# Earlier due times for the two variance transposes of an attention, and closer chunks in one normalisation

## The chip, the cores and the metric

The kernel runs on one core of a Trainium2 chip. The metric is the device time of one execution in microseconds (us). Before the change the median of three runs is 2762.81 us, and the runs lie between 2762.28 and 2766.79. All data is fp32.

## The reference

Eight images of 768 channels and 32x32 = 1024 tokens go through two residual layers. The core of it, shortened:

```python
def _L0_conv_ref(x, W_qkv, W_proj, b_proj):          # layer 0
    q, k, v = (qkv[0], qkv[1], qkv[2])               # 12 heads of 64
    var_v = jnp.var(v, axis=-1, ddof=1, keepdims=True)
    var_k = jnp.var(k, axis=-1, ddof=1, keepdims=True)
    scores = var_v @ jnp.swapaxes(var_k, -2, -1) * scale
    attn = jax.nn.softmax(scores, axis=-1)
    out = attn @ v
    out = out @ W_proj.T + b_proj
...
def _L1_conv_ref(feature, conv_w, conv_b):           # layer 1
    # 28 shifted products of the normalised features, summed over channels
    corr = jnp.stack([jnp.sum(feat_pad[:, :, r:h + r, cc:w + cc] * feat_n, axis=1) for r, cc in _offsets()], axis=1)
    x = jnp.concatenate([feature, corr], axis=1)
    out = jnp.einsum('bchw,oc->bohw', x, conv_w) + conv_b[None, :, None, None]
...
x = x + _L0_conv_ref(_gn(x), ...)                    # _gn: group norm, 32 groups
x = x + _L1_conv_ref(_gn(x), ...)
```

The queries are not used. A score is a product of one number for each query token (the head variance of v) and one for each key token (the head variance of k), so the attention needs no matmul for its scores: a row of value variances, spread over 128 partitions, goes through an exponential whose scale for each partition is a key variance.

## The kernel before

**The stages of an image.** The images are called 0 to 7. For each image the kernel runs: group norm; the projections to K and V, in two halves of six heads (`KeysValues`); the variances of each half (`spread`); the attention, in six pairs of heads, three to a half (`Pair`, `Attention`); the output projection with the residual and its statistics (`project`), which gives f; group norm of f; and layer 1 on f: the Gram products of the correlation (`Corr`, L1006) and the 1x1 convolution with its residual (`Conv`). Layer 1 of image b − 1 runs mixed with the attention of image b. The projections and the convolution are cut into units by a Strassen scheme, six matmuls each: 1.94 us for a unit of K and V, 2.57 us for one with a weight tile (wt) by TensorE's own records. In the profile the unit matmuls all stand at L342, since one helper issues them.

**The hand-over from projection to attention.** After the last unit of a half, `spread` works out, on VectorE (all of its instructions are recorded at L146), the scaled variance of k (km), its largest value (top, and most on GpSimd, L616) and that of v (vm), each 128 tokens by 48 (six heads by eight token tiles). Then two jobs follow.
- `values` calls `to_rows` on vm: TensorE transposes it (ptv, L501), VectorE copies it out (rsv), and the SyncE queue stores it to DRAM (vdr<-rsv, L504). From there `Pair.rows` loads one row for each head, spread over 128 partitions: bc<-vdr, 512 KB each, L665.
- `keys` computes nk, the key scale (six VectorE instructions). For the first half a job `rows` follows, 0.5 us after VectorE is free by the planner's count, which does the same for nk: ptk, rsk, kdr<-rsk, and bk<-kdr at L665.

**The attention of a pair.** For each of eight key tiles t and both heads, ScalarE computes ex = exp(bc · nk) (L674, 128x1024), and TensorE adds four products with v into av (L699), in blocks of four steps (32 records). The denominators come in one of two ways. For pairs 0, 1 and 2 ScalarE also computes exp(bk · vm) with a sum over its row (junk, L684); the sums are inverted (inv), transposed (it, L808), copied (ir), stored (di<-ir, L812) and loaded spread over partitions (rd<-di, L771). For pairs 3, 4 and 5 VectorE adds up the ex tiles (acc). From the second image on these three are the summed ones; in the first image pair 0 is one of them too. At last VectorE multiplies the finished pair by rd (v<-v,rd). There is one rd buffer, so the load for a pair waits until the pair before it is multiplied.

**What sets the order.** The program is written in one pass by a planner, `Clock`. `later.after(us, job)` puts a job at the planner's time plus us; `later.after_dve(us, job)` counts from the time at which the planner expects VectorE to be free. When the time comes, the job's instructions are appended to the engines' programs. These times are the planner's own and never wait on the chip: they only decide in which order each engine, and the SyncE queue with all of the large DMAs, runs its instructions. On the chip each engine runs its own list in that order, and between engines there are semaphores. The DMAs of the SyncE queue use eight completion semaphores in turn, so an issue also waits for the landing of the DMA eight issues before it.

**What stands around the hand-over of the second half.** Conv.start (L1103) loads the residual of layer 1 from DRAM in six row groups (x<-x1d), which are the accumulators of the convolution; VectorE's x<-x,bconv_sb,x and x<-y,bconv_sb,x add a unit's result and the bias to one. `thirds` and `fourth` of the convolution are the sums t2f, f<-f and t4f on VectorE. wt are the streamed weight tiles (L306, 196 KB), kv the ones of the projections (L279, 576 KB).

**What stands around it in the first half.** Gram products with their copies (win<-gr) and stores (windowed<-win, L1016) lie between the units of the second half. win copies, ptv, ptk and the inverse's transposes share the two PSUM buffers of the pool `smp`.

**The residual's normalisation.** `project` collects the group norm statistics of f. `apply` (inside it) calls `Norm.apply` (L457), which normalises the image in six chunks of 128x1024 (f<-f), each due `apart` us after the one before. Except for the last image f is overwritten in place, after a copy of each row group has been stored for layer 1's residual (x1d<-f).

Of the kernel before, what the change touches and what calls it, by code (L numbers as in the profile page):

```python
# [14 lines left out]
NB, C, H, W = 8, 768, 32, 32  # L15
# [136 lines left out]
def two_layers(ctx, tc, x, wkv, wproj, bproj, wconv, wcorr, bconv, out):  # L152
# [30 lines left out]
    later = clock  # L183
# [16 lines left out]
    def image_tile(pl, tag, name):  # L200
        return pl.tile([P, J, N], F32, tag=tag, name=name)
# [218 lines left out]
    def gn_tile(name):  # L420
        return st.tile([P, 2 * J, 6], F32, tag="bn", bufs=2, name=name)

    def gn_stats(bn, t, j, hf):
        vector.bn_stats(out=bn[:, 2 * j + hf, :], in_=t[:, j, hf * HF : (hf + 1) * HF])
# [61 lines left out]
    def head_m2(bn, m2, name):  # L486

        d = st.tile([P, MT * HH], F32, tag="hd", name=f"hd{name}")
        s = st.tile([P, MT * HH], F32, tag="hs", name=f"hs{name}")
        by_tile = [a.rearrange("p (t h) -> p t h", h=HH) for a in (d, s)]  # L490
        vector.tensor_tensor(d, bn[:, :, 1], bn[:, :, 4], ALU.subtract)
        vector.tensor_tensor(s, bn[:, :, 2], bn[:, :, 5], ALU.add)
        vector.tensor_tensor(d, d, d, ALU.mult)
        vector.scalar_tensor_tensor(
            m2.rearrange("p h t -> p t h"), by_tile[0], float(HD // 4), by_tile[1], ALU.mult, ALU.add
        )

    def to_rows(cols, dr, name):

        pt = small(f"pt{name}")  # L500
        nc.tensor.transpose(pt[0 : MT * HH, 0:P], cols.rearrange("p h t -> p (h t)"), ident)  # L501
        rs = work([MT * HH, P], f"rs{name}")
        vector.tensor_copy(rs, pt[0 : MT * HH, 0:P])
        nc.sync.dma_start(out=dr.rearrange("h (t p) -> (h t) p", p=P), in_=rs)  # L504

    class KeysValues:
# [47 lines left out]
        def unit(self, half, d, n, g, p):  # L554
            b = self.b
            if n == 0:
                self.make_sums(half, (2 * d, 2 * d + 1))
            s = self.sums[g]
            a = {1: self.block(g, 0, 0), 2: self.block(g, 0, 1), 4: self.block(g, 1, 1)}
            a.update({5: s[:, 0], 6: s[:, 1], 7: s[:, 2], 3: s[:, 3]})  # L560
            w = kv_stream.tiles[b, half, d, p]
            pairs = [(a[p][:, k, :], w[:, k, :]) for k in range(JH)]
            banks.product(g, p, KV_US, KW, pairs, lambda ps: self.take(half, g, p, ps))
            if p not in [q for _, q in PAIR[n + 1 :]]:
                kv_stream.done((b, half, d, p))
            if d == 1 and n == len(PAIR) - 1:
                self.over = half == 1
                later.after(KV_US + 0.5, lambda: later.after_dve(0.0, lambda: self.spread(half)))
# [39 lines left out]
        def spread(self, half):  # L608
            b = self.b
            name = f"{b}_{half}"  # L610
            km2 = st.tile([P, HH, MT], F32, tag="km2", bufs=2, name=f"km2{name}")
            head_m2(self.bn["k", half], km2, f"k{name}")
            top = st.tile([P, HH], F32, tag="top", name=f"top{name}")
            vector.tensor_reduce(top, km2, AX.X, ALU.max)
            most = st.tile([P, HH], F32, tag="most", name=f"most{name}")
            nc.gpsimd.partition_all_reduce(most, top, P, bass_isa.ReduceOp.max)  # L616
            m2 = st.tile([P, HH, MT], F32, tag="vm2", bufs=4, name=f"vm2{name}")
            head_m2(self.bn["v", half], m2, f"v{name}")
            nk = st.tile([P, HH, MT], F32, tag="nk", bufs=4, name=f"nk{name}")
            kdr, vdr = [dpool.tile([HH, N], F32, tag=f"{kind}dr", name=f"{kind}dr{name}") for kind in "kv"]  # L620
            for of, new in ((self.m2, m2), (self.nk, nk), (self.kdr, kdr), (self.vdr, vdr)):
                of.append(new)

            def values():
                to_rows(m2, vdr, f"v{name}")
                ready.add(("v", b, half))

            def keys():
                for h in range(HH):
                    vector.tensor_scalar(  # L630
                        nk[:, h, :], km2[:, h, :], most[:, h : h + 1], HD ** -0.5 / (HD - 1) ** 2,
                        ALU.subtract, ALU.mult,
                    )
                ready.add(("nk", b, half))
                if not set(SUMMED[b > 0]).issuperset(range(3 * half, 3 * half + 3)):
                    later.after_dve(0.5, rows)

            def rows():
                to_rows(nk, kdr, f"k{name}")
                ready.add(("k", b, half))  # L640

            later.after_dve(2.5, values)
            later.after_dve(3.5, keys)


    class Pair:
# [78 lines left out]
        def sum_up(self):  # L725
# [14 lines left out]
            def out():  # L740
                ds = denpool.tile([P, HF], F32, tag="den", name=f"ds{b}_{hp}")
                act_copy(0.55, ds, den)
                for at in range(4):
                    nc.sync.dma_start(
                        out=dr[0][at // 2 : at // 2 + 1, at % 2 * HF : (at % 2 + 1) * HF], in_=ds[32 * at : 32 * at + 1, :]
                    )
                later.after(6.0, spread)
# [437 lines left out]
    def project(b, ots):  # L1185
        f = first_f[0] if b == 0 else image_tile(fpool, "f", f"f{b}")
        for n, us in ((0, 0.0), (1, 0.5), (3, 1.5), (4, 3.0), (2, 12.0), (5, 14.0)) if b else ():
            later.after(us, lambda n=n: nc.sync.dma_start(out=f[:, n, :], in_=xv[b, :, n, :]))
        bn = gn_tile(f"bn2_{b}")
        if b + 1 < NB:  # L1190
            x1_dram[b] = dpool.tile([P, J, N], F32, tag="x1", name=f"x1d{b}")
        left = {(i, hf) for i in range(J) for hf in range(2)}

        def finished(i, hf):
            gn_stats(bn, f, i, hf)
            left.remove((i, hf))
            if b + 1 < NB and (i, 1 - hf) not in left:
                nc.sync.dma_start(out=x1_dram[b][:, i, :], in_=f[:, i, :])
            if not left:
                later.after(0.1, normalise)  # L1200

        def normalise():
            norm = Norm(bn, f"b{b}")
            later.after_dve(0.3, norm.means)
            later.after_dve(3.0, norm.spreads)

            def apply():
                to = f if b + 1 < NB else image_tile(xnpool, "xn", "f_last")
                layer1.append((to, f))
                norm.apply(to, f, ("f", b), 2.0 if b + 1 < NB else 0.0)  # L1210

            later.after_dve(5.0, apply)

        sums = TokenSums(f"o{b}", ots[:JH], ots[JH:])
        clock.wait(("ot", b, JH - 1), ready=ready)
        sums.first()
        wide = Wide("p", f"p{b}", f, bproj_sb, sums.operand, finished)
        late = True
        for n, (us, _, unit) in enumerate(wide.units()):
            if n == 4:  # L1220
                clock.wait(("ot", b, HP - 1), ready=ready)
            if late and n > 1 and ("ot", b, HP - 1) in ready:
                late = False
                sums.second()
                later.after(3.0, sums.thirds)
                later.after(8.0, sums.fourth)
            unit()
            clock.pass_time(us)
# [55 lines left out]
    for b in range(NB + 1):  # L1284
# [6 lines left out]
        if b:  # L1291
# [3 lines left out]
            f, acc = layer1[b - 1] if b > 1 else first_f * 2  # L1295
# [66 lines left out]
```

## Time and profile before

| what | value |
|---|---|
| median of the runs | 2762.81 us (2762.28 to 2766.79) |
| the profiled execution | 2773.49 us, of which its span is 2771.8 us |
| granted TensorE clock, mean | 0.993 |
| TensorE busy | 2712.3 us, 98% of the span |
| VectorE busy | 1664.1 us, 60% |
| ScalarE busy | 1362.3 us, 49% |
| GpSimd busy | 307.0 us, 11% |
| DMA moved | 451.85 MB, mean 163 GB/s |
| TensorE waiting for ex (av<-ex,v) | 12.3 us in 15 waits, the longest 5.0 us |

The span goes from the first to the last instruction of the profiled execution. Busy time counts the records of an engine; loading weights overlaps with matmuls and is counted apart. A line of a timeline gives start and duration in us from the span's start, engine, source line, operation, the tiles as out<-in, sizes, the number of records joined to it, and in brackets the idle time just before it and what ended that. A line of the SyncE queue (SPq) is a DMA's issue and not its landing. A line of the waits gives the engine, what it was about to run, what it waited for, and then the total, the number of waits and the longest.

### The profile page before, as it was taken

How to read it: one execution, taken by the hardware profiler on the slowest of the kernel's cores; microseconds unless marked ns; L12 is line 12 of the kernel's file. 1: busy time of each engine (PE TensorE's matmuls, PEld its weight loads, DVE VectorE, ACT ScalarE, POOL GpSimd, SP SyncE). 2: the span in 40 equal slices, each digit the busy share in tenths (PEclk: the TensorE clock that was granted, in tenths of full speed). 3: DMA queues.
4: the chain of work that ended last, by engine and by line, in shares of the span. 5: the costliest groups of instructions: out<-in, count | busy, mean ns of one | idle time of the engine just before them, and what ended most of it. 6: DMA issues, size and time to landing. Idle time of an engine off the chain costs nothing.

```text
span 2771.8 us, 28821 instructions
## 1 busy us (share of the span) xinstructions
PE 2712.3 (98%) x9063; PEld 1277.7 (46%) x9063; DVE 1664.1 (60%) x4163; ACT 1362.3 (49%) x1814; POOL 307.0 (11%) x350
## 2 busy tenths in 40 slices
PE   6999999999999999999999999999999999999999
PEld 3543454335643455434554346533465334653353
DVE  4858734685447854478534884358743587446853
ACT  1398078520596106970079701886019850298400
POOL 3420101002200031000310012100121001110000
PEclk9999999999999999999999999999999999999999
DMA  8764454545554545536456365563654536535323
GB/s 302 280 227 150 142 189 122 163 165 160 175 150 143 187 154 157 165 128 204 150 158 189 97 203 168 149 181 91 228 175 130 182 97 222 171 113 170 117 73 95
DMA packets 324579, 451.85 MB, mean 163 GB/s; under 512 B 59794, under 2 KB 245890, under 8 KB 324426
## 3 DMA queue, kind: packets, MB, share of 16 engines
q1 hardware_dynamic: 322618, 444.88, 50.8%
q10 hardware_dynamic: 1808, 5.11, 0.5%
q8 instruction: 73, 1.20, 0.2%
q14 instruction: 80, 0.66, 0.1%
HBM read 380.44 MB, written 67.38 MB: 162 GB/s over the span
## 4 chain that ended last, share of the span: by engine, by line
PE 74%; issue 10%; DMA 5%; ACT 5%; DVE 4%; SPq 1%; POOL 1%; DVEq 0%; POOLq 0%; ACTq 0%
PE x L342 29%; PE av L699 17%; PE y L342 14%; PE z L342 8%; ACT ex L674 3%; PE gr L1006 2%; DMA rd<-di 2%; ACT junk L684 2%; DMA bc<-vdr 1%; DVE dn L146 1%; PE den L732 1%; PE z L936 1%; PE x L936 1%; PE den L782 1%; DVE cs L146 0%
## 5 line engine op out<-in xcount | busy, mean ns | idle before, releaser
L674 ACT ACTIVATE ex<-bc,nk 128x1024 f32<-128x1024 f32 x768 | 834.5, 1138 | 493.6 <-DMA bc<-vdr 271.3
L699 PE MATMUL av<-ex,v 128*64 128x512 f32 x3072 | 709.1, 601 | 12.3 <-ACT ex L674 12.3
L684 ACT ACTIVATE junk<-bk,vm 128x1024 bf16<-128x1024 f32 x368 | 420.5, 1143 | 41.9 <-DMA bk<-kdr 35.6
L699 PEld LDWEIGHTS av<-ex,v 128*64 128x64 f32 x3072 | 218.7, 138 | 473.9 <-issue 394.4
L146 DVE TENSOR_TENSOR acc<-acc,ex 128x1024 f32<-128x1024 f32 x350 | 401.6, 1212 | 0.0
L209 ACT COPY kp<-x 128x384 f32<-128x384 f32 x28 | 13.3, 479 | 558.1 <-PE x L342 558.1
L342 PE MATMUL y<-kv,s 128*128 128x384 f32 x768 | 267.8, 489 | 2.6 <-DMA kv<-kvs 2.6
L342 PE MATMUL x<-kv,xn 128*128 128x384 f32 x768 | 263.9, 490 | 4.4 <-DVE xn L146 3.3
L342 PE MATMUL x<-kv,s 128*128 128x384 f32 x768 | 262.2, 489 | 3.3 <-POOL s L546 3.3
L342 PEld LDWEIGHTS x<-kv,xn 128*128 128x128 f32 x768 | 145.1, 191 | 108.6 <-issue 14.3
L342 PEld LDWEIGHTS x<-kv,s 128*128 128x128 f32 x768 | 145.4, 191 | 104.1 <-issue 6.8
L342 PEld LDWEIGHTS y<-kv,s 128*128 128x128 f32 x768 | 142.4, 190 | 102.1 <-issue 8.7
L1006 PE MATMUL gr<-f 128*128 128x227 f32 (+1 forms) x672 | 131.8, 346 | 0.0
L342 PE MATMUL z<-kv,xn 128*128 128x384 f32 x384 | 130.1, 488 | 0.0
L342 PE MATMUL x<-v,wt 128*128 128x512 f32 x288 | 130.0, 596 | 0.0
L1006 PEld LDWEIGHTS gr<-f 128*128 128x128 f32 x672 | 121.2, 190 | 18.7 <-issue 6.2
L146 DVE TENSOR_TENSOR v<-y,v 128x128 f32<-128x128 f32 x180 | 40.9, 282 | 136.5 <-PE y L342 136.5
L342 PE MATMUL x<-f,wt 128*128 128x512 f32 x252 | 115.4, 598 | 0.1
L452 POOL TENSOR_TENSOR rstda<-vea,neghalf 128x1 f32<-128x1 f32 x8 | 4.8, 597 | 930.2 <-DVE vea L146 930.2
L546 POOL TENSOR_TENSOR s<-xn 128x384 f32<-128x384 f32 x64 | 68.5, 1080 | 309.6 <-PE x L342 219.4
L146 DVE BATCH_NORM_STATS2 vbn<-v 128x6 f32<-128x64 f32 x720 | 101.7, 210 | 0.0
L146 DVE COPY acc<-ex 128x1024 f32<-128x1024 f32 x50 | 33.7, 703 | 107.6 <-ACT junk L684 36.8
(170 smaller groups left out, 2925.0 us busy)
## 6 DMA issues: line engine op xcount, KB each, us to landing
kv<-kvs SPq DMA_DIRECT2D x128, 576.0 KB
kv<-in_wkv_dram SPq DMA_DIRECT2D x96, 576.0 KB
bc<-vdr SPq DMA_DIRECT2D x96, 512.0 KB
f<-in_x_dram SPq DMA_DIRECT2D x48, 512.0 KB
bk<-kdr SPq DMA_DIRECT2D x46, 512.0 KB
x1d<-f SPq DMA_DIRECT2D x42, 512.0 KB
x<-x1d SPq DMA_DIRECT2D x42, 512.0 KB
out_dram<-x SPq DMA_DIRECT2D x84, 256.0 KB
```

Of the source, the lines that this page charges most:

```text
L146: return getattr(self.engine, name)(*args, **kw)
L209: nc.scalar.copy(to, at)
L342: nc.tensor.matmul(t, lhsT=lhsT, rhs=rhs, start=p in FIRST and k == 0, stop=stop and k == len(pairs) - 1, skip_group_check=True,)
L452: nc.gpsimd.tensor_tensor(self.rstd, ve, neghalf[:, 0:1], ALU.pow)
L546: nc.gpsimd.tensor_tensor(self.sums[g][:, 0], a[g][2], a[g][3], ALU.add)
L674: nc.scalar.activation(ex, self.bc[e], AF.Exp, scale=self.kv.nk[self.half][:, h, t : t + 1])
L684: nc.scalar.activation(junk, self.bk[e], AF.Exp, scale=self.kv.m2[self.half][:, h, t : t + 1], accum_out=self.sums[:, e, t : t + 1],)
L699: nc.tensor.matmul(self.av[e * HD : (e + 1) * HD, hf, :], lhsT=self.vt[:, t, e, :], rhs=exs[e][:, hf * HF : (hf + 1) * HF], start=t == 0, ...
L732: nc.tensor.matmul(den[at * 32 : (at + 1) * 32, :], lhsT=ones[:, 0:32], rhs=self.acc[e][:, hf * HF : (hf + 1) * HF], start=True, stop=True,)
L782: nc.tensor.matmul(den[e * HD : (e + 1) * HD, :], lhsT=ones, rhs=self.acc[e][:, at], start=True, stop=True)
L936: nc.tensor.matmul(t, lhsT=wcorr_sb[at, i, :], rhs=cs[at, tokens, :], start=False, stop=True, skip_group_check=True)
L1006: nc.tensor.matmul(ps[:, :n], lhsT=f[:, j, t * P : (t + 1) * P], rhs=f[:, j, t * P : t * P + n], start=j == 0, stop=j == J - 1,)
```

## The change

Three numbers change. `values` is due 1.0 us instead of 2.5 us after VectorE's expected end, and `keys` 2.2 us instead of 3.5 us, in all images but the first. And the six chunks of the residual's normalisation in `project` are due 1.0 us apart instead of 2.0 us where b is 0; b counts from 0, so this is the first image's residual. It is described in words as the second image's, whose layers run while that residual is used. The other images keep 2.0 us, and the last one 0.

```diff
@@ -639,8 +639,8 @@
                 to_rows(nk, kdr, f"k{name}")
                 ready.add(("k", b, half))
 
-            later.after_dve(2.5, values)
-            later.after_dve(3.5, keys)
+            later.after_dve(1.0 if b else 2.5, values)
+            later.after_dve(2.2 if b else 3.5, keys)
 
 
     class Pair:
@@ -1207,7 +1207,7 @@
             def apply():
                 to = f if b + 1 < NB else image_tile(xnpool, "xn", "f_last")
                 layer1.append((to, f))
-                norm.apply(to, f, ("f", b), 2.0 if b + 1 < NB else 0.0)
+                norm.apply(to, f, ("f", b), (2.0 if b else 1.0) if b + 1 < NB else 0.0)
 
             later.after_dve(5.0, apply)
```

No instruction is added or removed: every engine has the same number of instructions before and after, in another order.

## The prediction

> **What bounds the kernel now.** I read the busy times first: TensorE is busy 98% of the span.
>
> ```profile
> PE 2712.3 (98%) x9063; PEld 1277.7 (46%) x9063; DVE 1664.1 (60%) x4163; ACT 1362.3 (49%) x1814; POOL 307.0 (11%) x350
> ```
>
> The change adds and removes no instruction, so it can only move TensorE's idle and slow stretches. The view of what TensorE waited for shows how much there is:
>
> ```profile
> PE av L699 <- ACT ex L674: 12.3, 15, 5.0
> ...
> PE ct L1052 <- DVE dn L146: 5.2, 7, 3.1
> ...
> PE ptv L501 <- DVE vm L146: 1.8, 5, 0.5
> ```
>
> Only the first row belongs to the softmax hand-over, 12.3 us. It is too small, because a block that waits between its own records stretches them. A block of four steps (32 records, av) takes 7.02 us where nothing waits (image 4, 1440.80 to 1447.82). By TensorE's timeline the first block of pair 3 takes, start to next start, 15.06 (image 1), 10.51, 10.50, 10.63, 10.48, 8.81 and 8.27 us (images 2 to 7). Over 7.02 that is 8.04, 3.49, 3.48, 3.61, 3.46, 1.79 and 1.25, together 25.1 us; images 2, 3, 4 and 5 also start it 0.86, 1.6, 0.14 and 0.35 us late. This is the loss that the change can reach. TensorE, then VectorE, the DMA issues and ScalarE of image 4 show what makes it:
>
> ```profile
> 1501.07 0.29 PE L501 MATMUL ptv<-ident,vm 128*48 128x128 f32 x1 [0.41 <-DVE vm L146]
> ...
> 1520.56 6.08 PE L699 MATMUL av<-ex,v 128*64 128x512 f32 x22 [0.33 <-ACT ex L674]
> 1526.88 2.97 PE L699 MATMUL av<-ex,v 128*64 128x512 f32 x8 [0.24 <-ACT ex L674]
> ```
> ```profile
> 1503.00 0.75 DVE L146 SCALAR_TENSOR_TENSOR x<-x,bconv_sb,x 128x512 f32<-128x512 f32 x1 [1.99 <-DMA x<-x1d]
> 1503.67 1.88 DVE L146 TENSOR_TENSOR f<-f 128x512 f32<-128x512 f32 x3
> 1505.47 0.74 DVE L146 SCALAR_TENSOR_TENSOR x<-y,bconv_sb,x 128x512 f32<-128x512 f32 x1
> 1508.78 1.23 DVE L146 TENSOR_TENSOR v<-v,rd 128x1024 f32<-128x1024 f32 x1 [2.56 <-DMA rd<-di]
> 1509.92 0.28 DVE L146 COPY rsv<-ptv 48x128 f32<-48x128 f32 x1
> ```
> ```profile
> 1494.82 0.79 SPq L1103 DMA_DIRECT2D x<-x1d  x2
> 1495.73 0.57 SPq L306 DMA_DIRECT2D wt<-tsc  x1
> 1496.39 2.06 SPq L771 DMA_DIRECT2D rd<-di  x2
> ...
> 1510.22 0.33 SPq L504 DMA_DIRECT2D vdr<-rsv  x1
> 1510.61 0.42 SPq L1103 DMA_DIRECT2D x<-x1d  x1
> 1511.65 1.75 SPq L665 DMA_DIRECT2D bc<-vdr  x4
> ```
> ```profile
> 1517.95 1.15 ACT L674 ACTIVATE ex<-bc,nk 128x1024 f32<-128x1024 f32 x1 [5.63 <-DMA bc<-vdr]
> ```
>
> The transpose is done at 1501.4, but its copy (rsv) stands behind v<-v,rd of pair 1, which waits until 1508.78 for rd issued at 1496.39. So the value rows (vdr, then bc) go out 9 to 10 us late, ScalarE idles 5.63 us, and its first exponential, T = 1517.95, sets the block: its end is T + 11.8.
>
> [...] rsv, ready at 1501.4, ran at 1509.92. [...] rd (512 KB) issued at 1496.39 was usable at 1508.78, 12.4 us later, with the engines at 0.96 and 1.01 busy in 1496–1502 and 1502–1508. [...] The trace has it at image 1: after 5.04 us of idle eight av records take 4.71 us where the last eight above take 2.97. It also shows the same after the 2.1 us wait of image 3[...].
>
> **The change, part by part.** Values' due time falls by 1.5 us and keys' by 1.3 us for image 1 on; how far the instructions move I read from both kernels' order on each engine.
>
> *Half 1, images 2 to 7 (all alike).* ptv comes one weight unit earlier (2.57 us) but goes behind one block step more (1.74): 0.83 us net. With it pair 1's inverse (inv, ir, di) comes one unit earlier. On SP the two rd loads now precede the second of the paired x<-x1d above (x3, row group 3 of the image) and the wt behind it, and the four bc loads precede x2, the x<-x1d at 1510.61. On VectorE rsv stays behind v<-v,rd, and one x<-y eviction moves behind rsv and nk. So:
> - rd issues 2 to 3 us earlier, with about 0.7 MB (512 + 196 KB) less ahead; at some 250 GB/s (318 and 208 in the two windows) that is 2.9 us. rsv moves from 1509.92 to about 1507.
> - vdr follows (now +0.30 us), then 1.43 us to bc as before; x3 and wt, which rd overtook, are then in the rings, so I take bc at 1509.5 to 1510 instead of 1511.65; but x2's 512 KB is no longer ahead of it (1.6 to 2.1 us of landing at 318 to 250 GB/s).
> - T becomes 1514.5 to 1515.2: 2.8 us earlier (bounds 2 and 4; below nothing is the rival).
> - Per image the gain is the smaller of 2.8 and the loss less about 0.5 that later steps keep: 2.8, 3.2 (image 3 with the half clock after its wait), 2.8, 2.8, 1.3, 0.75 = 13.7 us. ptv's earlier place meets a vm that is no sooner, since it is behind x0's landing: +0.5 us per image before the block, absorbed while the exponentials decide.
>
> *Image 1.* ptv one unit earlier; rsv now stands before three f<-f and one x<-y, so it runs at about 488.1 instead of 490.49. bc issues 2.3 us earlier; rd of pair 2 (issued 503.52, waited for until 508.37) follows it in the rings. The 5.04 us stall shrinks by about 2 (1 to 4).
>
> *Half 0, images 2 to 7.* ptk is one half-unit earlier (1.94); SP puts the window store behind the bc loads and the two bk loads (1 MB) before a kv load. bk issues at about 1394.0 (behind rsk's store) instead of 1397.75, so ScalarE's wait goes:
>
> ```profile
> 1404.32 1.15 ACT L684 ACTIVATE junk<-bk,vm 128x1024 bf16<-128x1024 f32 x1 [3.92 <-DMA bk<-kdr]
> ```
>
> TensorE's first av blocks move up by half a unit too, which swaps equal work. They need one sum pass and the exponentials behind it, so bk must land by about 1402.9 (1404.32 less what block 0 gains, 1.94, with 0.5 of slack). Issue to use was 6.57 us before: 1400.5, margin 2.4. Image 5 loses 0.81 us there now and gains 0.8. ptk needs nk (ready about 1388.0) and the bank that the window copy frees (1388.35) when TensorE arrives at 1388.66: margin 0.3, so 0 to 0.2 us per image, +0.5 in all. If that cover is gone, each late tenth is paid six times.
>
> *The residual.* The code gives the 1.0 us gap where b is 0, which is the first image's residual: VectorE's six chunks of image 0 come interleaved closer, one waiting for the store x1d<-f (until 370.74, 2.05 us idle). VectorE then idles 8.15 us before its next operation at 379.70, and TensorE's order is the same: 0. Without that cover the cost is at most the 2 us of the wait.
>
> Sum: −13.7 − 2 − 0.8 + 0.5 = −16. The profiled execution took 2773.49 us for its span of 2771.8, 10.68 above the median of 2762.81; all terms are differences inside images, so I take them from the median: 2762.8 − 16 = **2747**.
>
> **Rivals.**
> - *The hand-over stays where it was* (no change). The DMA engines are full from 1496 to 1508; if rd's landing is set by the bytes issued long before it and by its own 2-row source, earlier issue only waits longer. For it: shares of 0.96 to 1.01. Against: what is moved behind it is 0.7 MB. Then only image 1 gains: 2761.
> - *The key rows become the bound* (slower). In the first half bk now follows directly on 2 MB of bc rows in full rings, 352 GB/s in 1391–1397 and share 1.00; 3 MB in a row take 8.9 us. If bk lands 12 us after issue as rd did, not 6.57, at 1406, it is 3.1 past 1402.9 less the slack above: about 2.5 us of stall, plus 2.3 for half clock, in each of six images: 29 − 16 = +13, 2776. It decides from 2.7 us per image (16/6), that is bk later than about 1405.6 without the clock, or 1403.5 with it. Against: issue comes 3.75 us earlier.
> - *Part of the gain comes back*: T moves only 1 to 1.5 us because the overtaken x3 and wt now hold up vdr and bc: 6 × 1.2 + 2 = 9, 2754. This lies inside the forecast's range.
> - *The residual part hurts*: a chunk waiting for x1d blocks VectorE beyond 380: at most +2 with the rest as forecast: 2749.
>
> **How the numbers follow.** A measurement of this kernel can tell 0.2% (5.5 us) from no change: the bounds are 2757.3 and 2768.3. Forecast with its partial form and the residual's rival: 0.66, own range 2740 to 2756 (the caps of the six losses, 17.4, with 4 at image 1, against ΔT of 1.2). No move: 0.18, 2758 to 2766. Key rows: 0.12, 2768 to 2785; another 0.04 is slower by ptk or ptv waits that are not absorbed. Faster 0.66, same 0.18, slower 0.16. For the range 2739 to 2767 I leave out the upper cases and 0.03 below.
>
> **What would show it.** Right: pair 3's first block at 7.3 to 8 us in images 2 to 7; ScalarE's first exponential after bc 15 instead of 16.9 us after ptv; v<-v,rd about 3 us sooner; no 3.9 us gap before junk; image 1's stall about 3 us. Wrong: av waits for ex in pair 0; a first junk later than 1405 in image 4's terms; waits of ptk for nk; rd landing 14 to 15 us after issue.

## The result: 0.28% faster, less than half of what was forecast

The changed kernel takes 2757.53 us (median of eight runs, 2753.73 to 2759.91), the kernel before 2764.61 us in the same comparison (eight runs, 2762.28 to 2767.63). The ratio is 0.9972 with a 95% interval of 0.9961 to 0.9983. That is 7.1 us, in the direction of the forecast and inside its range, where the sum had said 16. The profiled execution took 2754.9 us, with a span of 2753.2.

The busy line and the view of what TensorE waited for, of the changed kernel:

```profile
PE 2693.1 (98%) x9063; PEld 1273.7 (46%) x9063; DVE 1663.4 (60%) x4163; ACT 1355.5 (49%) x1814; POOL 305.6 (11%) x350
```
```profile
PE ptv L501 <- DVE vm L146: 8.5, 6, 2.1
PE av L699 <- ACT ex L674: 7.8, 4, 5.1
PE ct L1052 <- DVE dn L146: 3.9, 4, 3.1
```

The wait for ex has shrunk from 12.3 us in 15 waits to 7.8 in 4, and the longest of them is still image 1's. The wait at ptv has grown from 1.8 to 8.5 us. TensorE's timeline of image 4 has both:

```profile
1483.91 5.37 PE L699 MATMUL av<-ex,v 128*64 128x512 f32 x24
1491.19 0.29 PE L501 MATMUL ptv<-ident,vm 128*48 128x128 f32 x1 [1.90 <-DVE vm L146]
1491.41 1.94 PE L699 MATMUL av<-ex,v 128*64 128x512 f32 x8
...
1509.98 7.09 PE L699 MATMUL av<-ex,v 128*64 128x512 f32 x32
```

Pair 3's first block (the last line) now takes the 7.02 us of an undisturbed block up to its successor. The block ahead of it is cut by ptv, which waits 1.90 us for vm. VectorE, the queue and ScalarE of the same image:

```profile
1486.93 0.75 DVE L146 SCALAR_TENSOR_TENSOR x<-x,bconv_sb,x 128x512 f32<-128x512 f32 x1 [5.17 <-DMA x<-x1d]
...
1490.89 0.24 DVE L146 SCALAR_TENSOR_TENSOR vm<-hdv,hsv 128x48 f32<-128x48 f32 x1
1493.13 0.75 DVE L146 SCALAR_TENSOR_TENSOR x<-x,bconv_sb,x 128x512 f32<-128x512 f32 x1 [2.00 <-DMA x<-x1d]
1493.80 1.89 DVE L146 TENSOR_TENSOR f<-f 128x512 f32<-128x512 f32 x3
1495.60 1.22 DVE L146 TENSOR_TENSOR v<-v,rd 128x1024 f32<-128x1024 f32 x1
1496.73 0.28 DVE L146 COPY rsv<-ptv 48x128 f32<-48x128 f32 x1
```
```profile
1481.36 0.39 SPq L1103 DMA_DIRECT2D x<-x1d  x1
...
1484.26 1.48 SPq L771 DMA_DIRECT2D rd<-di  x2
...
1497.04 0.33 SPq L504 DMA_DIRECT2D vdr<-rsv  x1
1498.69 1.75 SPq L665 DMA_DIRECT2D bc<-vdr  x4
```
```profile
1502.80 6.54 ACT L674 ACTIVATE ex<-bc,nk 128x1024 f32<-128x1024 f32 x6 [2.10 <-DMA bc<-vdr]
```

v<-v,rd, which waited 2.56 us for rd before, follows its predecessor without a gap. The copy cs<-cs (a step of the correlation, issued at 1490.65 before and at 1480.43 now) stands in both kernels just ahead of the convolution's loads on the SyncE queue, so I count from it: the first exponential T comes 22.4 us after it, where it came 27.3 us after it. And vm stands behind the VectorE instruction that waits 5.17 us for the convolution's first load, issued at 1481.36 and used at 1486.93. That is what ptv meets.

### The profile page after: what moved, and what is told of

The parts are those of the page before. It is cut to its first block, busy times and chain, and to the rows that moved or that the text cites. A ratio compares the mean times of both kernels' runs of the same rounds, so it can differ in the third digit from the quotient of the medians.

```text
span 2753.2 us, 28842 instructions
## 1 busy us (share of the span) xinstructions
PE 2693.1 (98%) x9063; PEld 1273.7 (46%) x9063; DVE 1663.4 (60%) x4163; ACT 1355.5 (49%) x1814; POOL 305.6 (11%) x350
## 4 chain that ended last, share of the span: by engine, by line
PE 84%; issue 6%; DVE 4%; DMA 3%; ACT 2%; SPq 0%; POOL 0%; DVEq 0%; POOLq 0%; ACTq 0%
PE x L342 32%; PE av L699 21%; PE y L342 16%; PE z L342 9%; PE gr L1006 3%; DMA x<-x1d 1%; ACT ex L674 1%; DVE dn L146 1%; ACT junk L684 1%; PE den L732 1%; PE z L936 1%; PE x L936 1%; PE den L782 1%; PE y L936 1%; DVE cs L146 0%
## 5 line engine op out<-in xcount | busy, mean ns | idle before, releaser
L699 PE MATMUL av<-ex,v 128*64 128x512 f32 x3072 | 696.8, 600 | 7.8 <-ACT ex L674 7.8
L342 PEld LDWEIGHTS z<-kv,xn 128*128 128x128 f32 x384 | 72.3, 190 | 49.9 <-issue 3.0
```

Of the source, the lines that this page charges most:

```text
L342: nc.tensor.matmul(t, lhsT=lhsT, rhs=rhs, start=p in FIRST and k == 0, stop=stop and k == len(pairs) - 1, skip_group_check=True,)
L699: nc.tensor.matmul(self.av[e * HD : (e + 1) * HD, hf, :], lhsT=self.vt[:, t, e, :], rhs=exs[e][:, hf * HF : (hf + 1) * HF], start=t == 0, ...
```

## The experiments

The kernel before was profiled a second time, and eight variants ran beside it and the changed kernel. The table sums what TensorE lost over 7.02 us a block, in images 2 to 7, with losses under 0.15 us left out. A block is counted from its start to the start of what follows it; where ptv stands behind the block and not inside it, ptv and its wait are counted in. ct (L1052) is a transpose of the correlation that waits for dn of VectorE. "Image 1" is pair 3's first block there. The ratio compares each kernel with runs of the kernel before that were taken beside it (four groups, whose medians of the kernel before are 2762 to 2765 us); it is not the quotient of two medians, and medians of different groups can be compared to about 2 us only.

| kernel | pair 3, first block | block with ptv | pair 0, first block | pair 0, second block (ahead of ct before) | image 1 | median us | ratio (95%) |
|---|---|---|---|---|---|---|---|
| before, first profile | 17.1 | 4.6 | 0.8 | 2.5 | 8.0 | 2764.6 | 1 |
| before, second profile | 12.5 | 5.5 | 1.0 | 3.2 | 8.3 | 2757.5 (one run) | |
| changed | 0 | 12.8 | 2.6 | 0 | 8.1 | 2757.5 | 0.9972 (0.9961 to 0.9983) |
| no_residual | 0.5 | 13.2 | 3.1 | 0 | 7.8 | 2757.8 | 0.9978 (0.9972 to 0.9985) |
| second_half | 0 | 23.9 | 0.3 | 3.3 | 8.0 | 2765.3 | 1.0009 (1.0002 to 1.0017) |
| first_half | 0 | 1.4 | 5.8 | 0 | 8.1 | 2747.0 | 0.9941 (0.9929 to 0.9953) |
| keys_only | 6.7 | 0.9 | 4.0 | 0 | 10.1 | 2756.1 | 0.9970 (0.9958 to 0.9983) |
| x_behind_rd | 15.1 | 5.7 | 0.4 | 3.6 | 8.2 | 2763.3 | 1.0007 (0.9994 to 1.0020) |
| key_rows_first | 0.6 | 0.7 | 0 | 0 | 8.1 | 2742.6 | 0.9924 (0.9909 to 0.9940) |
| key_rows_and_inverse | 0 | 1.3 | 0 | 0 | 6.8 | 2743.4 | 0.9922 (0.9907 to 0.9937) |
| rd_after_sums | 0 | 0.8 | 0 | 0 | 0 | 2736.5 | 0.9893 (0.9875 to 0.9910) |

The columns are one profiled execution each, the medians are not, so they agree to a few us only. A 0 at pair 0's second block doesn't mean that the wait for dn is gone: in these kernels ct stands behind a projection unit instead, and in the changed kernel it still waits 0.9 us in images 2 to 7 together, where it waited 2.1 and 2.8 us in the two profiles of the kernel before.

**A second look at the kernel before.** No edit.

> The kernel before, unchanged, for a second profiled execution. The first one took 2773.5 us, 9 above the median of the runs. If that execution was an ordinary one whose excess lies outside the images (theory A: only the waits at ptv were mis-sized), pair 3's first blocks in images 2 to 7 lose about 17 us again. If the profile was an unlucky one (theory B: the loss to be had in an ordinary run is smaller than the profile showed), this execution takes 2762 to 2768 us and those blocks lose 8 to 12 us.

It took 2757.5 us. Pair 3's first blocks lost 12.5 us and none of them started late; in the first profile they had lost 17.1 and started 3.0 us late (0.86, 1.6, 0.14 and 0.35). The time is below what either theory gave, and the loss is just above theory B's 8 to 12: the first profile showed 7.6 us more to be gained than an execution 16 us faster had. The medians of the kernel before lie between the two, at 2762 to 2765, and single runs between 2755.65 and 2769.82. So the loss to be had differs from one execution to the next, as theory B said, though one more execution can't say what is ordinary. Whether the waits at ptv were mis-sized (theory A) is the next run's to say.

**The first half alone.**

```diff
-            later.after_dve(2.5, values)
-            later.after_dve(3.5, keys)
+            later.after_dve(1.0 if b and not half else 2.5, values)
+            later.after_dve(2.2 if b and not half else 3.5, keys)
```

> The earlier due times (1.0 and 2.2) only for the first half of images 1 to 7; the second half and the residual keep the old ones. TensorE then runs the second half's ptv one block step later (after step 7 of pair 2, not after step 6), while rd still goes ahead of the convolution's loads and bc ahead of the third of them. Theory A (the earlier ptv meets a vm that is not ready, and this gives back what the hand-over gained): no wait at ptv over 0.5 us, pair 3's blocks stay without loss, 2748 to 2751. Rival (the waits at ptv don't matter, the gain is small since the blocks of an ordinary run lose less): like the changed kernel, 2755 to 2759.

2747.0 us, 1 us below theory A's range, and the interval of its ratio does not touch the changed kernel's. TensorE's timeline of image 4: the block is whole, and ptv behind it waits 0.19 us.

```profile
1481.98 7.09 PE L699 MATMUL av<-ex,v 128*64 128x512 f32 x32
1489.26 0.29 PE L501 MATMUL ptv<-ident,vm 128*48 128x128 f32 x1 [0.19 <-DVE vm L146]
```

One step more of pair 2 ahead of ptv covers the wait, and T doesn't suffer (22.2 us after the copy of cs), since rsv is behind f<-f and v<-v,rd anyway. With both halves, but without the residual's part, the kernel takes 2757.8 us in the same group of runs (below). So the second half's part of the change, added to the first's, costs about 11 us: the first half's part alone is 15.6 us faster than before, both are 4.8 us faster by the medians of this group.

**The second half alone.**

```diff
-            later.after_dve(2.5, values)
-            later.after_dve(3.5, keys)
+            later.after_dve(1.0 if b and half else 2.5, values)
+            later.after_dve(2.2 if b and half else 3.5, keys)
```

> The earlier due times only for the second half of images 1 to 7. On VectorE rsv then stands before v<-v,rd of pair 1 instead of behind it, rd keeps its place behind the convolution's loads, and ptv comes one block step earlier than in the kernel before (after step 4 of pair 2, not 5). Theory A: ptv waits for vm, 2.1 us in each image; bc issues 3 us earlier, so pair 3's blocks gain about 2.8 us each and the ptv waits take back 1.8 each: 2756 to 2762. Rival (only rd's place on the queue frees the hand-over): no gain in pair 3, the waits at ptv come on top: 2768 to 2775.

2765.3 us, above the range of theory A (2756 to 2762) and below the rival's. Pair 3 did gain, all of its loss, as theory A said and the rival did not. The wait at ptv was sized rightly (2.1 us expected, 1.87 to 2.40 measured); what was left out is what follows it. TensorE in image 4:

```profile
1490.11 1.94 PE L699 MATMUL av<-ex,v 128*64 128x512 f32 x8
1494.44 0.29 PE L501 MATMUL ptv<-ident,vm 128*48 128x128 f32 x1 [2.40 <-DVE vm L146]
1494.66 7.07 PE L699 MATMUL av<-ex,v 128*64 128x512 f32 x24
```

The wait is 2.40 us, and then 24 records take 7.07 us where they take 5.37 in the changed kernel; the granted clock in 1496 to 1498 was 0.50. Over six images the waits are 13.0 us and the loss 23.9. So the two halves of the change do not add: the second alone gains the hand-over and pays a little more than that for it (2765.3 against 2762.6 us for the kernel before in the same group).

**Without the residual's part.** The changed kernel with this line as before:

```diff
-                norm.apply(to, f, ("f", b), (2.0 if b else 1.0) if b + 1 < NB else 0.0)
+                norm.apply(to, f, ("f", b), 2.0 if b + 1 < NB else 0.0)
```

> The changed kernel with the residual's chunks 2.0 us apart again, so both due times of the hand-over alone. Only VectorE's order in image 0 differs from the changed kernel. Forecast of the prediction: the residual part costs and gains nothing, 2755 to 2760, the same as the changed kernel. Rival (closer chunks hurt by up to 2 us because a chunk waits for the store x1d<-f): 2 us below it.

2757.8 us against 2757.5: no difference, as forecast. The two come from different groups of runs; their ratios, 0.9978 and 0.9972, lie inside each other's intervals.

**The keys alone.**

```diff
-            later.after_dve(3.5, keys)
+            later.after_dve(2.2 if b else 3.5, keys)
```

> Only keys at 2.2 (images 1 to 7, both halves); values and the residual as before. The attention is shifted and rd goes ahead as in the changed kernel, and ptv comes behind step 7 of pair 2, so it should not wait. Against the run with the first half alone one thing in the second half is different: x2 (512 KB) goes ahead of the four bc loads. Theory A (ptv's wait is what the changed kernel gives back): 2747 to 2751. If the place of bc ahead of x2 is worth the 2 us that the prediction gave it: first exponential 2 us later than there, part of the loss of pair 3 is back, 2751 to 2756.

2756.1 us, at the upper end of the second alternative. There are no waits at ptv (0.5 us in all), but 6.7 us of pair 3's loss are back, and the first exponential of image 4 comes 24.8 us after the copy of cs, against 22.2 with the first half alone. vdr is stored at the same time in both (16.65 us after the copy of cs), and bc issued at the same time (18.1 us), although nk stands ahead of rsv on VectorE here. What is left between them is x2: 512 KB ahead of bc on the queue are worth 2.5 us of T in this image. Over images 2 to 7 the time from the issue of bc to the first exponential is 0.8 to 2.5 us longer than with the first half alone, 1.75 us in the mean.

**One load behind rd.** The kernel before with x3 issued later; nothing moves on TensorE, VectorE or ScalarE.

```diff
-                for n, us in ((0, 0.0), (1, 1.0), (3, 2.5), (4, 4.0), (2, 12.0), (5, 14.0)):
+                for n, us in ((0, 0.0), (1, 1.0), (3, 4.5), (4, 5.0), (2, 12.0), (5, 14.0)):
```

> The kernel before with one thing moved: x3, the third of the convolution's loads (512 KB), is issued behind pair 1's rd and not ahead of it, in images 2 to 7 (in image 1, without such an rd, a weight tile passes one load). TensorE, VectorE and ScalarE keep the order of before. Prediction's step (the bytes ahead of rd in the rings set when it lands): v<-v,rd starts 2 us sooner, pair 3's blocks gain 1.5 us each, no wait at ptv is added: 2752 to 2756. Rival (rd is sooner only because pair 1 and its inverse end one unit sooner): as before, 2760 to 2765.

2763.3 us, no difference; but the reason is neither theory's. VectorE in image 4:

```profile
1499.86 0.75 DVE L146 SCALAR_TENSOR_TENSOR x<-y,bconv_sb,x 128x512 f32<-128x512 f32 x1 [1.82 <-DMA x<-x1d]
1500.52 1.22 DVE L146 TENSOR_TENSOR v<-v,rd 128x1024 f32<-128x1024 f32 x1
1501.66 0.28 DVE L146 COPY rsv<-ptv 48x128 f32<-48x128 f32 x1
```

rd is there in time: v<-v,rd has no gap. Now x<-y, the eviction that needs x3, waits 1.82 us in its stead and holds everything behind it. rsv runs 7.9 us after ptv, where it ran 8.9 after it before, and T stays (27.2 us after the copy of cs, 27.3 before). In the changed kernel this eviction stands behind rsv and nk on VectorE, so that the later x3 holds up nothing. So rd ahead of x3 gains nothing while the eviction stands ahead of rsv. What the eviction's move alone would gain was not tried.

**Key rows ahead of the second pair's value rows.** The first half alone, and in `load_rows` (hp and before are the pair and the one ahead of it):

```diff
-                    if ("c", e) not in pair.rows_at and (hp < 2 or self.pairs[hp - 2].passes["e"] == MT):
+                    if ("c", e) not in pair.rows_at and (hp < 2 or self.pairs[hp - 2].passes["e"] == MT) and not (
+                        hp == 1 and not before.summed and ("k", 1) not in before.rows_at
+                    ):
```

> The first half's due times as in the run with the first half alone, and on the queue pair 0's key rows (bk, 1 MB) ahead of pair 1's value rows (bc, 1 MB). Nothing else moves. The prediction's rival of the key rows was right in its mechanism if pair 0's first block waits for the sum passes that need bk: its loss (0.85, 1.81, 0.72, 0.66, 0.45 and 1.35 us in images 2 to 7 there, 5.8 together) then goes: 2741 to 2744. If those blocks wait for something else: unchanged, 2746 to 2748. If pair 1's rows come too late: slower.

2742.6 us, as the first alternative had it, and in TensorE's timeline the 5.8 us are gone. (The two times come from different groups of runs, and the intervals of their ratios overlap a little, so the gain in time is less sure than the timeline.) ScalarE of image 3, first with the first half alone, then with the key rows first:

```profile
1045.10 6.57 ACT L674 ACTIVATE ex<-bc,nk 128x1024 f32<-128x1024 f32 x6 [27.73 <-DMA bc<-vdr]
1056.41 1.15 ACT L684 ACTIVATE junk<-bk,vm 128x1024 bf16<-128x1024 f32 x1 [4.74 <-DMA bk<-kdr]
```
```profile
1042.59 6.55 ACT L674 ACTIVATE ex<-bc,nk 128x1024 f32<-128x1024 f32 x6 [27.46 <-DMA bc<-vdr]
1050.39 1.15 ACT L684 ACTIVATE junk<-bk,vm 128x1024 bf16<-128x1024 f32 x1 [1.24 <-DMA bk<-kdr]
```

The first sum pass comes 7.8 us after the first exponential and not 11.3, and pair 0's first block no longer waits. Pair 1's rows, behind, are in time.

**Image 1's stall, by the inverse's place.** The kernel above, and:

```diff
-            later.after_dve(3.5, self.spread)
+            later.after_dve(1.0 if (self.b, self.hp) == (1, 2) else 3.5, self.spread)
```

> As the run with the key rows first, and in image 1 alone pair 2's inverse is transposed one unit sooner, so that its store (di) is issued 4 loads sooner and rd of pair 2 ahead of a load and a weight tile. The prediction took image 1's 5 us stall to shrink with bc. If instead it is rd of pair 2 that ends it (store of di to load of rd took 8 us, and v<-v,rd waited 8.7 us), the stall of 5 us with its 2.4 us at half clock goes for the most part: 4 to 7 us less than the run with the key rows first. If bc or the exponentials bound it: no difference; if v<-v,rd, now ahead of two evictions on VectorE, blocks them: up to 3 us more.

2743.4 us, no difference to 2742.6. v<-v,rd of pair 2 came 2.1 us sooner (26.3 instead of 28.4 us after the copy of cs), and the block's loss fell from 8.1 to 6.8 us only. The stall seems to follow rd, but moving the inverse brings rd too little sooner to show in the time.

**Image 1's stall, by VectorE's queue.** The kernel with the key rows first, and the planner's guess of when rd lands, which sets the place of v<-v,rd:

```diff
-            self.rd_at = clock.now + 6.0
+            self.rd_at = clock.now + (14.0 if (self.b, self.hp) == (1, 2) else 6.0)
```

> As the run with the key rows first, with one VectorE instruction moved: in image 1 alone v<-v,rd of pair 2 comes eight sums (acc) later. The stall of pair 3's first block in image 1 (8.1 us, unchanged by the change) is then explained as a queue behind an operand: v<-v,rd waits 9 us for rd of pair 2, the sums behind it hold the ex tiles, and ScalarE has none free. If so, the block's loss falls from 8.1 to under 2 us: 2735 to 2738. If the exponentials are late for another reason (bc, the store of di, the DMA): 2741 to 2744.

2736.5 us, 6.0 below the run that it starts from, and the whole 8.1 us of loss is gone. VectorE and then ScalarE of image 1, first with the key rows first, then with the one instruction moved:

```profile
503.09 1.23 DVE L146 TENSOR_TENSOR v<-v,rd 128x1024 f32<-128x1024 f32 x1 [9.07 <-DMA rd<-di]
504.23 1.29 DVE L146 COPY acc<-ex 128x1024 f32<-128x1024 f32 x2
...
505.01 7.43 ACT L674 ACTIVATE ex<-bc,nk 128x1024 f32<-128x1024 f32 x7 [6.76 <-DVE acc L146]
```
```profile
497.26 1.29 DVE L146 COPY acc<-ex 128x1024 f32<-128x1024 f32 x2
498.79 6.90 DVE L146 TENSOR_TENSOR acc<-acc,ex 128x1024 f32<-128x1024 f32 x6 [0.25 <-ACT ex L674]
506.43 1.23 DVE L146 TENSOR_TENSOR v<-v,rd 128x1024 f32<-128x1024 f32 x1 [0.73 <-DMA rd<-di]
...
496.57 13.63 ACT L674 ACTIVATE ex<-bc,nk 128x1024 f32<-128x1024 f32 x13 [0.68 <-DMA bc<-vdr]
```

The sums, which free the ex tiles, stood behind an operand that was 9 us late, and ScalarE waited 6.76 us for them. Ahead of it they fill that time, and ScalarE runs on. This version, which has neither the second half's nor the residual's part of the change, beats both kernels: its ratio to the kernel before is 0.9893 (0.9875 to 0.9910), and the medians lie 25.7 us apart.

## Why the prediction was right in direction and wrong in size

**The bound and the chain** were right: TensorE's losses in pair 3, made by rsv behind v<-v,rd behind rd. The chain was undersized. T was to come 2.8 us sooner, although the step's own parts add up to 3.3 to 4.3 us (bc 1.7 to 2.2 sooner, x2's place 1.6 to 2.1). In image 4 it came 4.9 sooner than in the first profile of the kernel before (27.3 to 22.4 us after the copy of cs), of which 2.7 lie ahead of the issue of bc and 2.2 behind it; in the second profile T was at 25.7. All of the loss went, not all but 0.5 a block. That the bytes issued ahead of a load set when it lands was the author's estimate there. For x2's place it came out about rightly: the keys alone put it at 0.8 to 2.5 us, 1.75 in the mean. The step named the eviction that moves behind rsv and gave it no price; the run with one load behind rd shows that rd ahead of x3 gains nothing without it.

**"+0.5 us per image before the block, absorbed while the exponentials decide"** is the step that failed most. It is not consistent with its own sum: the same change takes the exponentials away as the thing that decides, so that nothing is left to absorb it. And its size was off: 1.2 to 1.4 us an image more were lost in these blocks than in the two profiles of the kernel before, not 0.5. ptv meets vm 0.9 to 2.05 us late in images 2 to 7 instead of 0.1 to 0.45: in image 4, counted from the issue of the convolution's first load, TensorE arrives 0.6 us sooner (7.9 us, 1481.36 to 1489.29, where it was 8.6, 1492.09 to 1500.66), and the load takes 5.6 us from issue to use (1481.36 to 1486.93) where it took 4.7 (1492.09 to 1496.80). The blocks with ptv lost 12.8 us where they had lost 4.6: 6.7 us of longer waits and 1.5 of slower records behind them. The first half alone, without those waits, reached what the prediction had forecast for the whole change, 2747.0. That the two numbers agree so closely is in part luck: pair 0 lost 5.8 us there, which the forecast didn't have either.

**"All terms are differences inside images, so I take them from the median"** was not safe either. The first profiled execution was 8.9 us above the median, and a part of its excess lay in the very losses that the change removes: 20.1 us with the late starts, against 12.5 in the second profile, so 7.6 of the 16 us between the two executions. The rest lay elsewhere, 3.2 us of it in the first projections of image 0. This did little harm, since the prediction had limited its gain in these blocks to 13.7 us. Against the second profile the terms are −12.5 at pair 3, +7.3 at ptv, +1.6 at pair 0, −0.2 in image 1 and −1.9 of waits at ct: −5.7. Against the first they are −20.1, +8.2, +1.8, 0 and −1.2: −11.3. The 7.1 us between the medians lie between the two sums; the three executions themselves took 2773.5, 2757.5 and 2754.9 us, since they also differ where the change does nothing. The term at ct was not in the prediction.

**Image 1's −2** did not come: 8.04 us of loss became 8.06. rsv ran sooner as said, but vdr to bc took 3.1 us there (485.75 to 488.89) and not the 1.43 carried over from image 4, so bc came 0.5 us sooner; and bc was not the bound. rd of pair 2 was, through the sums behind it, as the last run shows.

**Half 0** was wrong in one number. bk was to be issued 3.75 us sooner, right behind the store of nk. Before, it stood on the queue behind a kv load that was issued at 1397.07. Now it comes first, but it waits until the store of nk has landed, 6.7 us after that was issued (1380.25 to 1386.92 in image 4): the queue's view of waits gives bk 25.3 us of waiting for kdr, where it gave 3.5 before. So bk came 11.4 us after ptv, where it had come 11.1 after it, and ScalarE's wait for it, which was to go, was 4.1 us. The first blocks, half a unit sooner, then meet it: 2.6 us lost instead of 0.8. The rival of the key rows was right that bk would bind these blocks, but not in its reason, a landing 12 us after issue: bk was used 5.4 us after its issue, and it was the issue that came late. At 2.6 us in six images the effect is also far below the 2.7 us an image from which it would have decided. No wait at ptk is in the view of waits.

**The residual** costs nothing, as said. Of the rivals the first (no move) and the fourth are refuted by pair 3's block and by the run without the residual's part; the third, a part given back, names the right outcome with a wrong cause: vdr and bc were not held up (1.65 us between them in image 4, against 1.43), ptv was.

**A reading of the trace.** The prediction speaks of a 2.1 us wait in image 3 ahead of slow records. The view shows waits of 1.55 and 0.21 us there, and then records of 1.06 us, where undisturbed ones have 0.59, at a granted clock of 0.50 (1183 to 1185). It also set 4.71 us for eight records of image 1 against 2.97; eight that wait for nothing take 1.94. The 2.3 us for half clock in the rival of the key rows were an estimate: eight records lost 2.77 us in image 1 of the kernel before, after a wait of 5.04 us (4.71 against 1.94), and 1.61 us in image 6 of the changed kernel, after one of 2.05 (3.55 us against 1.94).

## What to carry to other kernels

When a change takes a stall away, price every delay that the stall used to hide, since its cover goes with it (here 0.5 us an image, called absorbed, became 1.2 to 1.4). Take the size of a loss from more than one profiled execution, above all where the profiled one is slower than the median (20.1 and 12.5 us here). And ask of each instruction in an engine's list which operand it waits for and what stands behind it: in image 1 moving v<-v,rd, which waited 9.07 us for rd, behind sums that were ready gained the whole 8.1 us of loss, and bringing rd 2.1 us sooner gained nothing that shows in the time (2743.4 us against 2742.6).

## What was not expected of the hardware

- The store of 48 rows (vdr, 24 KB) was followed by its loads 1.4 to 1.7 us later in images 2 to 7 of the kernel before and of the changed one, and 3.6 to 4.8 us later with the second half alone (14.48 to 19.27 us after the copy of cs in image 5), where it is issued sooner after the convolution's loads. The queue's view of waits has 29.3 us of bc waiting for vdr there, and 9.3 us in the kernel before. Sooner issue was therefore partly lost. That the loads ahead of the store hold it up fits this, but no run tested it.
- TensorE ran slow records after some waits of about 2 us and not after others. In the changed kernel the waits at ptv of 0.91 to 1.90 us (five images) were each followed by eight records in 1.94 us, and the one of 2.05 us (image 6, below) by eight in 3.55, at a granted clock of 0.50 in 2164 to 2166. With the second half alone a wait of 2.40 us was followed by slow records (image 4, above). The length alone doesn't decide: in image 3 of the kernel before records of 1.06 us came after waits of 1.55 and 0.21 us, at a clock of 0.50 in 1183 to 1185. And in image 0 a wait of 3.33 us in the kernel before was followed by twelve records in 5.80 us (clock 0.64 in 34.87 to 38.87), one of 3.43 us at the same place of the changed kernel by twelve in 4.11 us (clock 1.00 in 35.03 to 39.03). What decides was not shown.

```profile
2162.61 0.29 PE L501 MATMUL ptv<-ident,vm 128*48 128x128 f32 x1 [2.05 <-DVE vm L146]
2162.84 3.55 PE L699 MATMUL av<-ex,v 128*64 128x512 f32 x8
```
